# An encoder-decoder layer with cross attention: rows centred by ScalarE, and all copies of turned probabilities on ScalarE

## The chip, the core and the metric

The kernel runs on one core of a Trainium2 chip. A core has five engines that run their own queues of instructions in order and wait for each other by semaphores: TensorE (PE in the profile, with its weight loads as PEld), VectorE (DVE), ScalarE (ACT), GpSimd (POOL) and SyncE (SP), which here only issues transfers. Matrix products and transposes of TensorE land in PSUM, which has eight banks of 128 x 512 floats; everything else lives in SBUF, 128 partitions wide. The metric is the device time of one execution in microseconds, taken as the median of several runs.

## What is computed

Two batches of one encoder layer over 77 context rows and one decoder layer over 2048 rows, width 512, 16 heads of 32, feed-forward width 2048, all in float32:

```python
x = src                                    # (2, 77, 512)
x = x + mha(ln(x, n1), ln(x, n1), enc_in, enc_out, rel_bias)
x = x + relu(ln(x, n2) @ ff1.T + b1) @ ff2.T + b2
memory = x
y = tgt                                    # (2, 2048, 512)
y = y + mha(ln(y, n1), ln(y, n1), sa_in, sa_out, rel_bias + causal)
y = y + mha(ln(y, n2), memory, ca_in, ca_out, cross_bias)     # the cross attention
h = ln(y, n3)
y = y + relu(h @ ff1.T + b1) @ ff2.T + b2

def ln(x, s, b):
    m = mean(x); v = mean((x - m) ** 2)    # over the 512 of a row
    return (x - m) * rsqrt(v + 1e-6) * s + b
```

The change touches two norms of the decoder, n2 ahead of the cross attention and n3 ahead of the feed-forward part, and the softmax probabilities of the cross attention.

## The kernel before

The decoder's rows are cut into eight blocks of 512 (two batches of four), and each block into four tiles of 128 rows. The first part of the span, to about 1757 us, is causal self-attention with the encoder's stages between its units; in its second half (about 923 to 1215 us) the cross attention of block 0 is put between the units as well (`first_cross`). From there on runs the feed-forward part, 56 slots a block. In every slot the generator `cross(x + 1)` first adds its stages for the next block, and then `ff_slot` adds 1/56 of this block's feed-forward products. The first 28 slots of a block are `first_product`, the others `second_product`; both use Strassen-like sums of sub-matrices, so that VectorE and GpSimd add and subtract 128 x 512 pieces (`minus`, L1090, and others) while TensorE multiplies.

The order of instructions is written out by hand: no scheduler moves anything, so each engine executes its part of the program in the order in which the program emits it. An engine whose next instruction waits holds back all of its later ones.

**The norms.** `norm_stages` gives three stages for a tile of rows. `stats` lets VectorE take mean and variance (L740, L741), add epsilon (L742), and GpSimd raise the sum to the power -1/2 (L743). `center` has VectorE subtract the mean and multiply by that factor (L749), from the rows `y` in SBUF into a spare tile `xn`; then GpSimd adds to `y`, in place, the bias row of the coming product (L750). `turned` has TensorE transpose `xn` into one PSUM bank (L755) and ScalarE apply scale and shift on the way to SBUF, four 128 x 128 pieces (L758). In `cross`, the three stages of tile t of n2 are in the slots t, t + 2 and t + 4; q products (`q_group`, L765) follow in slots 9 to 12. For n3, they are 13, 15 and 17 slots after the slot where the tile's attention starts, 14 + 7t. At slot 0, `sums_n` also puts four sums (L1090) on GpSimd.

**The attention of a tile.** `attend_stages` gives scores (L780, four PSUM banks, then L789 and L790 on VectorE), exp (L793), sums (L798, L799), the normalization on GpSimd (L804), `turned`, the product with v (L821, copied by L825), and the output product (L830, added to y by L831). `turned` transposes the 16 heads' probabilities into four banks (L810, 16 transposes), and copies each bank to SBUF: two by VectorE (L812) and two by ScalarE (L814), in turns. In the feed-forward part only four banks rotate for all of this, because the other four hold the feed-forward products, so the scores of the next tile, one slot on, use the same banks again.

**The feed-forward evacuations** share the queues: `first_product` ends with a copy by ScalarE (L1313), or with an addition by VectorE (L1316), and for a finished piece two relus by ScalarE (L1319). ScalarE's copy L1340 and VectorE's L1341 and L1346 to L1348 belong to `second_product`, with GpSimd's additions L1351 and L1270 beside them.

Of the kernel before, what the change touches and what calls it, by code (L numbers as in the profile page):

```python
# [10 lines left out]
F32 = mybir.dt.float32  # L11
AF = mybir.ActivationFunctionType
ALU = mybir.AluOpType
# [4 lines left out]
P = 128  # L18
B, T, S, D = 2, 2048, 77, 512
# [35 lines left out]
def tile_encoder_decoder(ctx: ExitStack, tc: tile.TileContext, ins, out):  # L55
    nc = tc.nc
# [20 lines left out]
    def vec(name, i):  # L77
        c = _COL[name] + i
        return vecs[:, c : c + 1]
# [78 lines left out]
    with (  # L158
# [20 lines left out]
        def bank():  # L179

            i = count["bank"] % count["banks"]
            count["bank"] += 1
            return psum[:, i, :]
# [6 lines left out]
        def rows4(r):  # L190
            return slice(r * HD, (r + 1) * HD)
# [540 lines left out]
        def norm_stages(y, n, row, place, done):  # L732

            keep = {}

            def stats():
                st = sm.tile([P, 6], F32, name="bnst", tag="bnst")
                mv = sm.tile([P, 2], F32, name="cmv", tag="cmv", bufs=4)
                rs = sm.tile([P, 2], F32, name="crs", tag="crs", bufs=4)
                nc.vector.bn_stats(st, y())  # L740
                nc.vector.bn_aggr(mv, st)  # L741
                nc.vector.tensor_scalar_add(rs[:, 0:1], mv[:, 1:2], EPS)  # L742
                nc.gpsimd.tensor_tensor(rs[:, 1:2], rs[:, 0:1], mhalf[:, 0:1], ALU.pow)  # L743
                keep.update(mv=mv, rs=rs)

            def center():
                xn = keep["xn"] = place()
                mv, rs = keep["mv"], keep["rs"]
                nc.vector.tensor_scalar(xn, y(), mv[:, 0:1], rs[:, 1:2], ALU.subtract, ALU.mult)  # L749
                nc.gpsimd.tensor_tensor(y(), y(), row, ALU.add)  # L750

            def turned():
                xn, pt, dst = keep["xn"], bank(), done()
                for c in range(NC):
                    nc.tensor.transpose(pt[:, ts(c, P)], xn[:, ts(c, P)], ident)  # L755
                for c in range(NC):
                    sc, bi = vec(f"dec_{n}_s", c), vec(f"dec_{n}_b", c)
                    nc.scalar.activation(dst[:, c, :], pt[:, ts(c, P)], AF.Identity, bias=bi, scale=sc)  # L758

            return stats, center, turned  # L760
# [7 lines left out]
        def attend_stages(q, kTc, v, y, biased, pr, pts, place, w_o, bi=None):  # L768


            prh = pr.rearrange("p (h k) -> p h k", k=S)
            by_r = pr.rearrange("p (g r k) -> p g r k", r=HC, k=S)
            keep = {}

            def score():
                mx = sm.tile([P, NC, HC], F32, name="cmx", tag="cmx", bufs=3)
                banks = [bank() for _ in range(HC)]
                for g in range(NC):
                    for r in range(HC):
                        nc.tensor.matmul(  # L780
                            banks[r][:, ts(g, S)], q(g)[rows4(r)], kTc[rows4(r), g, :], start=True, stop=True
                        )
                for r in range(HC):
                    s = banks[r][:, : NC * S].rearrange("p (g k) -> p g k", k=S)
                    d = by_r[:, :, r, :]
                    if biased:
                        nc.vector.tensor_tensor(d, s, bi[r] if bi else d, ALU.add)
                        s = d
                    nc.vector.tensor_reduce(mx[:, :, r], s, AX.X, ALU.max)  # L789
                    nc.vector.tensor_tensor(d, s, mx[:, :, r, None].to_broadcast([P, NC, S]), ALU.subtract)  # L790

            def exp():
                nc.scalar.activation(pr, pr, AF.Exp)  # L793

            def sums():
                su = sm.tile([P, H], F32, name="csu", tag="csu", bufs=2)
                ri = sm.tile([P, H], F32, name="cri", tag="cri", bufs=2)
                nc.vector.tensor_reduce(su, prh, AX.X, ALU.add)  # L798
                nc.vector.reciprocal(ri, su)  # L799
                keep["ri"] = ri  # L800

            def normalize():
                ri = keep["ri"]
                nc.gpsimd.tensor_tensor(prh, prh, ri[:, :, None].to_broadcast([P, H, S]), ALU.mult)  # L804

            def turned():
                for g in range(NC):
                    pt = bank()
                    for r in range(HC):
                        nc.tensor.transpose(pt[:S, ts(r, P)], prh[:, g * HC + r, :], ident)  # L810
                    if g % 2:
                        nc.vector.tensor_copy(pts(g), pt[:S, :])  # L812
                    else:
                        nc.scalar.copy(pts(g), pt[:S, :])  # L814

            def times_v():
                ot = bank()
                for g in range(NC):
                    for r in range(HC):
                        h = g * HC + r  # L820
                        nc.tensor.matmul(  # L821
                            ot[rows4(r), ts(g, P)], v[:, ts(h, HD)], pts(g)[:, ts(r, P)], start=True, stop=True
                        )
                keep["oT"] = place()
                nc.scalar.copy(keep["oT"], ot)  # L825

            def out():
                mm, oT = bank(), keep["oT"]
                for c in range(NC):
                    nc.tensor.matmul(mm, oT[:, ts(c, P)], w_o[:, c, :], start=(c == 0), stop=(c == NC - 1))  # L830
                nc.vector.tensor_tensor(y(), mm, y(), ALU.add)  # L831

            return score, exp, sums, normalize, turned, times_v, out

        def first_cross():
# [713 lines left out]
```

## Time and profile before

| what | us |
|---|---|
| median of 3 runs | 2880.58 (2879.85 to 2881.13) |
| the profiled execution, its time | 2880.44 |
| the profiled execution, its span | 2878.70 |
| TensorE busy | 2827.8 |
| VectorE busy | 2033.3 |
| ScalarE busy | 1296.5 |
| GpSimd busy | 737.3 |
| L749, centring on VectorE, 64 of them | 0.54 to 1.53 each |
| L812, copies on VectorE, 64 of them | 0.68 each |
| L814, copies on ScalarE, 64 of them | 0.57 to 0.58 each |
| L743, the power on GpSimd, 64 of them | 0.54 to 1.11 each |

Durations and moments come from one profiled execution; moments are counted from the start of its span. A row in order of time reads: start, duration, engine, line, operation, output and inputs with the buffers' names, shapes, and how many instructions were merged into the row; in brackets how long the engine sat idle before it, and what ended that. A row of waits reads: engine and line that waited, the engine and line it waited for, the total in us, how often, and the longest. Durations of neighbours on one engine may overlap by some hundredths of a us. What `DVE pts L749` or `DVE xt L749` names is the same line with another spare tile for its output.

### The profile page before, as it was taken

Reading aid. Unit: us, or ns where it says so; the run is one execution under the profiler, and the core shown is the slowest. Engines: PE = TensorE matmul, PEld = TensorE weight load, DVE = VectorE, ACT = ScalarE, POOL = GpSimd, SP = SyncE. Lnnn points to the kernel's source line nnn. Section 1 sums busy time; section 2 is a strip of 40 time slices with the busy share of each in tenths; the row PEclk is TensorE's granted clock in tenths of the full one; section 3 lists DMA queues with packets and bytes.
Section 4 is the critical chain, followed back from the end, with each engine's and each line's share of the span. In section 5 each row is a group of like instructions: output and inputs, shape, how many; then the busy total and the mean of one; then the engine's idle time right before and its main releaser. Section 6 shows DMA issues by size and latency. Waiting matters only on the chain.

```text
span 2878.7 us, 64333 instructions
## 1 busy us (share of the span) xinstructions
PE 2827.8 (98%) x25782; PEld 2041.2 (71%) x25782; DVE 2033.3 (71%) x5550; ACT 1296.5 (45%) x2455; POOL 737.3 (26%) x573
## 2 busy tenths in 40 slices
PE   9899999999999999999999999999999999999998
PEld 5557666666666556666666677888888888888888
DVE  4767688878986678788878894666666666666645
ACT  3344465456665446555546674323232323232321
POOL 0100050200000101020000002363636363636355
PEclk9899999999999999999999999999999999999999
DMA  6413443401111502232301115454546454545365
GB/s 174 116 32 123 122 135 101 121 18 45 35 42 57 143 23 68 71 105 69 89 16 38 38 35 188 131 182 130 182 131 198 130 182 131 181 132 180 116 201 182
DMA packets 251773, 316.16 MB, mean 110 GB/s; under 512 B 29472, under 2 KB 142672, under 8 KB 251346
## 3 DMA queue, kind: packets, MB, share of 16 engines
q1 hardware_dynamic: 251474, 312.05, 35.9%
q8 instruction: 203, 3.33, 0.5%
q14 instruction: 96, 0.79, 0.1%
HBM read 273.07 MB, written 38.90 MB: 108 GB/s over the span
## 4 chain that ended last, share of the span: by engine, by line
PE 81%; DVE 8%; POOL 4%; ACT 3%; issue 3%; DMA 1%; SPq 0%; POOLq 0%; DVEq 0%; ACTq 0%
PE psum L425 17%; PE psum L371 11%; PE psum L1303 10%; PE psum L442 9%; PE psum L1332 7%; PE psum L765 4%; PE psum L215 4%; PE psum L239 4%; PE psum L251 4%; PE psum L226 3%; PE psum L830 3%; DVE pp L1090 2%; PE psum L780 1%; PE psum L810 1%; ACT pp L402 1%
## 5 line engine op out<-in xcount | busy, mean ns | idle before, releaser
L402 ACT ACTIVATE pp<-pp,nm 128x128 f32<-128x128 f32 (+15 forms) x512 | 611.6, 1201 | 265.6 <-DVE nm L397 265.3
L380 DVE TENSOR_SCALAR_CACHE_REDUCE pp<-psum 128x512 f32<-128x512 f32 (+3 forms) x1024 | 559.2, 590 | 58.2 <-PE psum L371 56.7
L425 PEld LDWEIGHTS psum<-ident,pp 128*128 128x128 f32 x4352 | 475.3, 142 | 110.1 <-DVE pp L380 50.8
L425 PE MATMUL psum<-ident,pp 128*128 128x128 f32 x4352 | 537.6, 278 | 8.3 <-DVE mx L387 3.8
L431 ACT COPY pts<-psum 128x512 f32<-128x512 f32 (+3 forms) x592 | 298.1, 575 | 474.9 <-PE psum L425 368.8
L429 DVE COPY pts<-psum 128x512 f32<-128x512 f32 (+2 forms) x544 | 330.0, 659 | 68.2 <-PE psum L425 67.9
L371 PE MATMUL psum<-kT,q 32*128 32x512 f32 (+3 forms) x2560 | 362.4, 578 | 7.1 <-ACT pts L431 4.5
L442 PEld LDWEIGHTS psum<-pts,vv 128*32 128x32 f32 x8704 | 227.3, 110 | 126.1 <-issue 117.3
L1332 PE MATMUL psum<-pp 128*128 128x128 f32 x2560 | 306.4, 276 | 1.9 <-POOL pp L1090 1.6
L1332 PEld LDWEIGHTS psum<-pp 128*128 128x128 f32 x2560 | 295.8, 192 | 17.4 <-issue 10.6
L442 PE MATMUL psum<-pts,vv 128*32 128x128 f32 x8704 | 280.9, 277 | 0.7 <-ACT pts L431 0.6
L1303 PE MATMUL psum<-vv,pp 128*128 128x256 f32 x1024 | 238.5, 381 | 0.0
L371 PEld LDWEIGHTS psum<-kT,q 32*128 32x128 f32 x2560 | 125.7, 184 | 143.6 <-issue 88.6
L1303 PEld LDWEIGHTS psum<-vv,pp 128*128 128x128 f32 x1024 | 189.8, 190 | 32.2 <-issue 8.4
L387 DVE CUSTOM_DVE_ANT_0 pp<-psum,bias 128x256 f32<-128x256 f32 (+1 forms) x512 | 195.9, 411 | 16.4 <-PE psum L371 16.4
L1090 POOL TENSOR_TENSOR pp<-pp 128x512 f32<-128x512 f32 x124 | 171.6, 1399 | 105.2 <-DMA pp<-in_dec_ff_wT_dram 91.2
L285 POOL TENSOR_TENSOR rstd<-rstd,mhalf 128x1 f32<-128x1 f32 x32 | 18.2, 570 | 668.1 <-DVE rstd L284 668.1
L1319 ACT ACTIVATE kT<-kT,vecs 128x256 f32<-128x256 f32 x192 | 87.7, 508 | 219.3 <-DVE kT L1316 219.2
L1303 PE MATMUL psum<-nT,pp 128*128 128x256 f32 x768 | 173.4, 379 | 0.0
L1303 PEld LDWEIGHTS psum<-nT,pp 128*128 128x128 f32 x768 | 145.3, 190 | 28.6 <-issue 10.2
L804 POOL TENSOR_TENSOR oT<-oT,cri 128x1232 f32<-128x1232 f32 x28 | 67.7, 2418 | 353.8 <-DVE cri L799 353.8
L1316 DVE TENSOR_TENSOR kT<-kT,psum 128x512 f32<-128x512 f32 x96 | 65.7, 686 | 119.1 <-PE psum L1303 89.7
(188 smaller groups left out, 3703.9 us busy)
## 6 DMA issues: line engine op xcount, KB each, us to landing
pp<-w_d SPq DMA_DIRECT2D x520, 256.0 KB, 2.9
pp<-in_dec_ff_wT_dram SPq DMA_DIRECT2D x112, 256.0 KB, 3.8
wqk<-in_dec_sa_in_wT_dram SPq DMA_DIRECT2D x64, 256.0 KB, 3.7
bias<-tzg SPq DMA_DIRECT2D x128, 128.0 KB, 3.7
wbig<-in_dec_sa_in_wT_dram SPq DMA_DIRECT2D x8, 1024.0 KB, 6.6
vv<-in_enc_ff_wT_dram SPq DMA_DIRECT2D x8, 1024.0 KB, 5.3
wbig<-in_dec_sa_out_wT_dram SPq DMA_DIRECT2D x8, 1024.0 KB, 6.6
vv<-y SPq DMA_DIRECT2D x32, 256.0 KB, 5.5
```

The costliest lines, as they stand in the source:

```text
L215: nc.tensor.matmul(mm, w[:, c, :], nTs[b, m][:, c, :], start=(c == 0), stop=(c == NC - 1))
L371: nc.tensor.matmul(banks[r][:, : kn * P], q[rows4(r), ts(t, P)], kT[rows4(r), g, k0 * P : (k0 + kn) * P], start=True, stop=True,)
L380: nc.vector.tensor_scalar(p[:, k0 * P : (k0 + far) * P], s[:, : far * P], 1.0, None, ALU.mult, ALU.max, accum_out=st["mx"][:, r, c : c + 1],)
L387: nc.vector.tensor_tensor_reduce(p[:, (i + 1) * P - w : (i + 1) * P], s[:, far * P : kn * P], biases[b, m, g][:, r, 2 * P - w :], 1.0, LOW ...
L402: nc.scalar.activation(p, p, AF.Exp, bias=nm, accum_out=to)
L425: nc.tensor.transpose(pt[:, ts(x, P)], state[n]["p"][r][:, ts(k, P)], ident)
L429: nc.vector.tensor_copy(pts[:, : len(load), :], pt[:, :w])
L431: nc.scalar.copy(pts[:, : len(load), :], pt[:, :w])
L442: nc.tensor.matmul(ot[rows4(r), t, :], vv[:, k, ts(g * HC + r, HD)], got.pop((n, k, r)), start=(k == 0), stop=(k == i),)
L1090: engine.tensor_tensor(out, a, b, ALU.subtract)
L1303: nc.tensor.matmul(mm[:, ts(f, TOK)], a[:, c, ts(f, P)], b[:, c, :], start=fresh and f == 0 and c == 0, stop=c == 1, skip_group_check=True,)
L1332: nc.tensor.matmul(psum[:, bank_i, ts(col, P)], lhs[:, c, :], w[:, c, :], start=fresh and k in (0, 3) and c == 0, stop=c == 3, skip_group_ ...
```

## The change

`stats` now has GpSimd compute a third column after the power, minus the mean times the factor, in one instruction of one column. `center` is now a ScalarE activation, the identity with a scale (the factor) and a bias (that third column) for each row, in VectorE's place; the two forms give the same value, (x - m) r = x r + (-m r). GpSimd's addition to `y` thus waits for ScalarE's reading of `y`. In `turned` of the attention all four copies are ScalarE's. All else is as it was; later lines move up or down by up to two (the centring is L750, the new multiplication L744, the copies L812 in the changed kernel, GpSimd's row addition L751, evacuations L759, relus L1317 and copies L1311 of the feed-forward part).

```diff
             def stats():
...
-                rs = sm.tile([P, 2], F32, name="crs", tag="crs", bufs=4)
+                rs = sm.tile([P, 3], F32, name="crs", tag="crs", bufs=4)
                 nc.vector.bn_stats(st, y())
                 nc.vector.bn_aggr(mv, st)
                 nc.vector.tensor_scalar_add(rs[:, 0:1], mv[:, 1:2], EPS)
                 nc.gpsimd.tensor_tensor(rs[:, 1:2], rs[:, 0:1], mhalf[:, 0:1], ALU.pow)
-                keep.update(mv=mv, rs=rs)
+                nc.gpsimd.tensor_scalar(rs[:, 2:3], mv[:, 0:1], rs[:, 1:2], -1.0, ALU.mult, ALU.mult)
+                keep.update(rs=rs)
 
             def center():
                 xn = keep["xn"] = place()
-                mv, rs = keep["mv"], keep["rs"]
-                nc.vector.tensor_scalar(xn, y(), mv[:, 0:1], rs[:, 1:2], ALU.subtract, ALU.mult)
+                rs = keep["rs"]
+                nc.scalar.activation(xn, y(), AF.Identity, bias=rs[:, 2:3], scale=rs[:, 1:2])
                 nc.gpsimd.tensor_tensor(y(), y(), row, ALU.add)
...
                     for r in range(HC):
                         nc.tensor.transpose(pt[:S, ts(r, P)], prh[:, g * HC + r, :], ident)
-                    if g % 2:
-                        nc.vector.tensor_copy(pts(g), pt[:S, :])
-                    else:
-                        nc.scalar.copy(pts(g), pt[:S, :])
+                    nc.scalar.copy(pts(g), pt[:S, :])
```

## The prediction

> **What bounds the kernel now.** I read the page's busy shares and its chain first, then what TensorE (PE) waited for, then instructions in order of time around those waits.
>
> ```profile
> span 2878.7 us, 64333 instructions
> PE 2827.8 (98%) x25782; PEld 2041.2 (71%) x25782; DVE 2033.3 (71%) x5550; ACT 1296.5 (45%) x2455; POOL 737.3 (26%) x573
> ...
> PE 81%; DVE 8%; POOL 4%; ACT 3%; issue 3%; DMA 1%; SPq 0%; POOLq 0%; DVEq 0%; ACTq 0%
> ```
>
> TensorE is busy for 98%, so the change is worth what it does to TensorE's 51 us of idle time, not what it moves between VectorE (DVE) and ScalarE (ACT). What TensorE waited for, in total us, times and longest, between 1860 and 2770 us:
>
> ```profile
> PE psum L755 <- DVE xt L749: 6.5, 9, 1.1
> PE psum L755 <- DVE pts L749: 3.0, 4, 1.1
> PE psum L780 <- DVE pts L812: 2.3, 7, 0.3
> ```
>
> Both edited lines stand here: 9.5 us for the centring (L749), 2.3 us for the copies (L812). 11.8 us is all that the change can take away directly. The order in time, one block of the feed-forward part (blocks repeat every 143.9 us):
>
> ```profile
> 2036.48 0.66 PE L755 MATMUL psum<-ident,pts 128*128 128x128 f32 x4 [0.44 <-DVE pts L749]
> ...
> 2064.72 0.60 PE L755 MATMUL psum<-ident,xt 128*128 128x128 f32 x4
> ...
> 2068.14 0.66 PE L755 MATMUL psum<-ident,pts 128*128 128x128 f32 x4 [1.08 <-DVE pts L749]
> 2068.63 1.89 PE L1303 MATMUL psum<-vv,pp 128*128 128x256 f32 x8
> 2070.36 0.60 PE L755 MATMUL psum<-ident,xt 128*128 128x128 f32 x4
> ```
> ```profile
> 2034.36 0.54 POOL L743 TENSOR_TENSOR crs<-crs,mhalf 128x1 f32<-128x1 f32 x1
> ...
> 2060.41 0.55 POOL L743 TENSOR_TENSOR crs<-crs,mhalf 128x1 f32<-128x1 f32 x1
> 2060.92 1.27 POOL L1090 TENSOR_TENSOR vv<-nT 128x512 f32<-128x512 f32 x1
> 2062.27 1.33 POOL L1090 TENSOR_TENSOR vv<-nT,vv 128x512 f32<-128x512 f32 x1
> ...
> 2066.02 0.55 POOL L743 TENSOR_TENSOR crs<-crs,mhalf 128x1 f32<-128x1 f32 x1
> 2066.53 1.26 POOL L750 TENSOR_TENSOR vv<-vv,row_sa_bv 128x512 f32<-128x512 f32 x1
> ```
> ```profile
> 2069.74 0.91 ACT L1319 ACTIVATE kT<-kT,vecs 128x256 f32<-128x256 f32 x2 [4.70 <-DVE kT L1316]
> 2070.55 1.49 ACT L758 ACTIVATE pp<-psum,vecs 128x128 f32<-128x128 f32 x4
> 2071.92 0.59 ACT L1313 COPY kT<-psum 128x512 f32<-128x512 f32 x1
> ```
>
> The reader sees a 1.08 us wait in the norm ahead of the queries (n2, second of four row tiles): GpSimd (POOL) reaches the power at 2066.02 only, after four sums of 1.27, VectorE centres after it, TensorE transposes after that. This form occurs in six blocks (6 x 1.08 = 6.5); the other 3.0 us are 0.43 in each of seven blocks, in the norm after the attention (n3, third tile), again behind a late power, at 2034.36. So what bounds both places is GpSimd, and the centring is the last link.
>
> **Part 1, VectorE's centring goes (64 x L749).** By line it takes 0.54 us at least, 1.45 in the median of those from vv. VectorE's own work hides behind TensorE; the gain is the last link only: 1.48 us at 2066.60, with 0.03 from the power's end to it and 0.06 from its end to the transposes.
>
> **Part 2, ScalarE's centring.** No row has it. ScalarE's exp with one per-partition operand takes 390 ns at 128x128 and 710 at 128x512 (groups by shape), so 0.32 us more for 384 columns; L758 with two such operands takes 475 (median, 128x128). 475 + 320 = 0.80 us. Ends: 0.59 (L1313's copy of 128x512) and 1.23 (exp over 128x1232). I take 0.80, the two rows with the same operands. The last link is 0.65 us shorter.
>
> **Part 3, GpSimd's extra multiplication (64, on 128x1, right after the power).** The trace has none. Nearest by shape is the power itself, 0.55; the other end is the page's memset of 128x1, 0.10. It needs the power's result: dependent GpSimd instructions leave a gap (the sum at 2062.27 starts 0.08 after its input's end at 2062.19), independent ones overlap by 0.03, so 0.11 more. I take 0.55 + 0.11 = 0.66; the low end is 0.21. It is in GpSimd's queue ahead of the four sums too, and of the row additions L750, which now wait for ScalarE's reading instead of VectorE's.
>
> **Part 4, n2 worked out.** GpSimd: tile 0's multiplication stands before the sums, tile 1's behind its power, so tile 1's factor comes at 2066.57 + 2 x 0.66 = 2067.89. Centring to 2068.72, transposes at 2068.78. TensorE is ready at 2068.14 - 1.08 = 2067.06: wait 1.72.
> ScalarE's queue in the changed program is: centre 1, the pair of relus (0.81 to the next), four evacuations L758 of tile 0 (1.37), centre 2, a copy (0.49), four evacuations of tile 1, centre 3. The relus and evacuations behind centre 1 now wait for GpSimd with it. Centre 2 can start by this queue at 2067.92 + 0.72 + 0.81 + 1.37 = 2070.82 (0.72 because neighbours overlap by some 0.08). Its factor: the row addition of tile 0 from 2068.72 (1.26), power, multiplication: 2071.15. It ends at 2071.95, transposes 2072.01; TensorE is ready 2.22 after the last transposes (2068.14 to 2070.36), at 2071.00: wait 1.01. Centre 3 starts 0.72 + 0.49 + 1.37 later, at 2073.73, transposes at 2074.59, ready at 2074.23: wait 0.36.
> Sum 3.09 against 1.08: +2.01 in six blocks, **+12.1**. What is late next: the query products L765 waited 0.12 for the last evacuation (2076.58 to 2076.70); TensorE now arrives later than ScalarE, **-0.7** in six.
> With the low end, 0.21: waits 0.82, 0.68 and 0.36, +0.78 in six, +4.7. So even a nearly free multiplication leaves n2 no faster.
>
> **Part 5, n3.** Third tile: power's end 2034.90 + 0.66 + 0.03 + 0.80 + 0.06 = 2036.45, ready at 2036.04: wait 0.41 instead of 0.44, **-0.2** over seven; with 0.21 the wait goes, -3.0. The other three tiles have their centred rows 1 us and more ahead (the nearest, the fourth: power's end 2048.46, rows 2050.0, transposes 2051.12). ScalarE idles there (4.35 us before L825 at 2034.12), so L825 behind the centring slips by 2.2 us, to 2036.3; its reader L830 starts at 2038.76.
>
> **Part 6, the copies (64 x L812 to ScalarE).** 0.58 us each (L814), 0.49 apart when queued; TensorE makes a bank in 0.49. So ScalarE ends 0.8 us behind the last transpose, and the next scores L780 come 1.7 us behind it: the seven waits go, **-2.3**. Where a relu is in front (1842.90, two L814 in 1.22) the four end 0.6 us before L780.
>
> **Part 7, the first block, inside self-attention.** 8 x 0.80 + 8 x 0.57 = 11 us more on ScalarE between 923 and 1215 us: 0, since ScalarE idles 3 to 10 us ahead of most groups there and TensorE waits for neither line. 11 us if that cover were gone; VectorE's relief brings no more than the 4.3 us that TensorE waited in that stretch at all. Table, DMAs and SP's queue are unchanged.
>
> **Sum.** 12.1 - 0.7 - 0.2 - 2.3 = +8.9 with the multiplication at 0.55; 4.7 - 0.7 - 3.0 - 2.3 = -1.3 at 0.10. The profiled execution took 2880.44 (span 2878.7 and 1.74 around it), the median is 2880.58, so either base serves: 2889.3, and 2879.1 at the low end. I forecast 2889, by the row of the same engine and shape.
>
> A rule speaks against the row I chose. The Trainium skill, GPSIMD Engine Reference, section Instruction dispatch, puts the cost of entering an instruction at tens of cycles, so the power's 0.55 would be mostly its arithmetic, and a product of one column would cost an estimated 0.1 us. By that the sum is -1.3; no row here shows such a product.
>
> **Rivals.**
> *Cheap multiplication, no change.* The two ends give 10.2 us for 0.45 us of multiplication, 23 us per us; so at 0.10 to 0.40 us the sum lies between -1.3 and +5.6. For it: GpSimd's sums of 384 columns take 1.007 and of 512 take 1.27, which leaves 0.22 at no column; against: the only 128x1 arithmetic takes 0.55. Time 2882.
> *Faster.* Mechanism: ScalarE's centring in n2 is so short that its queue keeps up. The three waits are 3 x centring + 2 x (multiplication with gap) - 0.96; with 0.21 they fall below today's 1.08, and the total below -5.8, once the centring is under 0.55. At 0.50 the total is -6.6: 2874. For it: ScalarE's 256-column relu from SBUF takes 0.51. Against: exp over 512 takes 0.71 with one operand fewer.
> *Much slower.* ScalarE's waiting for GpSimd reaches the exponentials in the first block: all of its 11 us, on top of +8.9: 2900. Against: there the factor is ready a slot earlier, GpSimd idling 8 to 10 us at a time.
>
> **How the numbers follow.** A measurement here tells about 0.2% (5.8 us) from no change. Forecast +6 to +14: 0.44; much slower 0.06; cheap multiplication 0.38; faster 0.12. So slower 0.50, same 0.38, faster 0.12. The forecast's own range is 2886.4 to 2894. The range that leaves out 2 in 10 reaches through the cheap case (2879, and some 4 us for what I charged nothing) to half of the faster one at 2875, and up to 2895.
>
> **What would show it.** TensorE's waits for L812 gone; L755 waiting for ScalarE (L750 there) in n2 at the second, third and fourth tile, 1.7, 1.0 and 0.4; the new L744 on GpSimd at about 0.55; ScalarE waiting for GpSimd some 2 to 3 us at tile 1. Wrong if L744 takes 0.2 or less, if the centring differs from 0.80, or if L755 waits only at the second tile.

## The result, and the profile after

| | us |
|---|---|
| before, median of the runs beside it (7 each) | 2881.13 (2877.09 to 2882.96) |
| after, median | 2870.03 (2868.08 to 2871.86) |
| ratio, with its 95% interval | 0.9963 (0.9951 to 0.9975) |
| after, the profiled execution and its span | 2870.03 and 2868.2 |

The change makes the kernel 0.37% faster: 2880.58 x 0.9963 is 10.7 us less. The forecast was 2889, 8 us slower, and its range began at 2875. From the page of the kernel after, the head, the busy shares and the chain that ended last:

```profile
span 2868.2 us, 64539 instructions
...
PE 2821.6 (98%) x25782; PEld 2036.2 (71%) x25782; DVE 1930.3 (67%) x5422; ACT 1371.7 (48%) x2583; POOL 741.8 (26%) x637
...
PE 90%; DVE 3%; ACT 3%; POOL 2%; DMA 1%; issue 1%; SPq 0%; POOLq 0%; DVEq 0%; ACTq 0%
```

VectorE gave up 103 us of work, ScalarE took over 75, and TensorE is still busy for 98% of the span. Its own busy time fell by 6.2 us, although it executes the same 25782 instructions: part of the gain hides in what the profile calls busy. What TensorE waited for between 1860 and 2770 us, in total us, times and longest:

```profile
PE psum L756 <- ACT xt L750: 7.1, 12, 1.1
PE psum L756 <- ACT pts L750: 3.6, 6, 1.1
```

The waits for the copies are gone, and the waits for centred rows add up to 10.7 where they were 9.5. By this view alone the change would be worth 1.1 us. The norm ahead of the queries (n2) in the same block as before, TensorE in order of time:

```profile
2060.70 0.60 PE L756 MATMUL psum<-ident,xt 128*128 128x128 f32 x4
...
2064.12 0.66 PE L756 MATMUL psum<-ident,pts 128*128 128x128 f32 x4 [1.08 <-ACT pts L750]
...
2067.00 0.66 PE L756 MATMUL psum<-ident,xt 128*128 128x128 f32 x4 [0.50 <-ACT xt L750]
...
2069.58 0.66 PE L756 MATMUL psum<-ident,xt 128*128 128x128 f32 x4 [0.19 <-ACT xt L750]
...
2073.53 3.60 PE L766 MATMUL psum<-pp,wqk 128*128 128x512 f32 x8
```

There are three waits now, where there was one. On GpSimd, the power, the new product, and the row addition that follows:

```profile
2062.30 0.55 POOL L743 TENSOR_TENSOR crs<-crs,mhalf 128x1 f32<-128x1 f32 x1
2062.95 0.27 POOL L744 TENSOR_SCALAR crs<-cmv,crs 128x1 f32<-128x1 f32 x1
2063.17 1.27 POOL L751 TENSOR_TENSOR vv<-vv,row_sa_bv 128x512 f32<-128x512 f32 x1
```

The product takes 0.27, with a gap of 0.10 ahead of it (the power ends at 2062.85). From a power's start to the next instruction it is 0.87 now and was 0.51 (2066.02 to 2066.53), so the product costs GpSimd's queue 0.36. And ScalarE's queue:

```profile
2063.25 0.81 ACT L750 ACTIVATE pts<-vv,crs 128x512 f32<-128x512 f32 x1 [2.37 <-POOL crs L744]
2063.97 0.89 ACT L1317 ACTIVATE kT<-kT,vecs 128x256 f32<-128x256 f32 x2
2064.77 1.48 ACT L759 ACTIVATE pp<-psum,vecs 128x128 f32<-128x128 f32 x4
2066.14 0.81 ACT L750 ACTIVATE xt<-vv,crs 128x512 f32<-128x512 f32 x1
```

The centring takes 0.81. The second one starts at 2066.14, 0.8 us after GpSimd has its factor (the product of 2065.05 ends at 2065.32): here ScalarE's queue is the last link, with the relus and evacuations that queued up behind the first centring's wait.

**Where the time went.** Up to the start of the feed-forward part the two profiled executions agree (1757.41 before, 1756.80 after). From there to the end, before took 1121.3 us and after 1111.4, 9.9 less. The waits as printed don't add up to that, so each place is measured by TensorE's steps: from the start of one group of matmuls to the start of a later one, against the same stretch where nothing waits.

The largest term is at the scores of each block's fourth tile, which take the banks that hold the third tile's turned probabilities. Before, TensorE in order of time:

```profile
2153.78 0.44 PE L780 MATMUL psum<-pts,bias 32*128 32x77 f32 x2
2154.56 0.45 PE L780 MATMUL psum<-pts,bias 32*128 32x77 f32 x4 [0.34 <-DVE pts L812]
2155.16 1.11 PE L780 MATMUL psum<-pts,bias 32*128 32x77 f32 x26
2156.20 2.05 PE L1332 MATMUL psum<-pp 128*128 128x128 f32 x16
```

After, the same place:

```profile
2150.51 1.13 PE L781 MATMUL psum<-pts,bias 32*128 32x77 f32 x32
2151.57 1.60 PE L1330 MATMUL psum<-pp 128*128 128x128 f32 x12
```

The 32 matmuls of one tile take 1.06 us to the next group in the kernel after, and took 2.42 before: the stall was 1.36, of which the profile printed 0.34 as idle. The rest stood in the rows as busy time: the three rows add up to 2.00, while 32 matmuls in one run take 1.13. The likely reason is that each time a wait cuts the group, the passage of the matmuls last issued stands as busy time of its own, where in one run it lies under the next ones. The view of groups had it, before and after (busy us, mean ns, then idle us with what ended it):

```profile
L780 PE MATMUL psum<-pts,bias 32*128 32x77 f32 x896 | 37.7, 279 | 3.4 <-DVE pts L812 2.3
```
```profile
L781 PE MATMUL psum<-pts,bias 32*128 32x77 f32 x896 | 31.7, 277 | 0.0
```

The 896 matmuls of this shape are busy for 6.0 us less, which is part of the gain, and their idle time falls from 3.4 to 0.0.

Why the copies were late is in VectorE's queue of the kernel before, in order of time:

```profile
2147.39 5.18 DVE L1090 TENSOR_TENSOR pp<-pp,kT 128x512 f32<-128x512 f32 x3
2152.49 0.41 DVE L1341 TENSOR_TENSOR oT<-psum,oT 128x256 f32<-128x256 f32 x1
2152.83 0.68 DVE L740 BATCH_NORM_STATS2 bnst<-vv 128x6 f32<-128x512 f32 x1
...
2153.83 1.27 DVE L812 COPY pts<-psum 77x512 f32<-77x512 f32 x2
```

The transposes into the four banks had ended at 2152.07. But three sums held VectorE to 2152.5, and the statistics of n3's second tile came next, so the two copies ran at 2153.83 to 2155.10, while TensorE wanted those banks for scores at 2153.78.

| per block, feed-forward part | before | after | times | us |
|---|---|---|---|---|
| scores of the fourth tile, start to next group | 2.42 | 1.06 | 7 | -9.5 |
| n3's third tile, step into its transposes | 2.49 | 1.88 | 7 | -4.3 |
| n2, first to fourth tile's transposes | 7.80 | 8.88 | 6 | +6.5 |
| n2, last transposes to the query products | 4.18 | 3.95 | 6 | -1.4 |
| end of the fourth tile's scores to its transposes L810 | 14.32 | 14.25 | 7 | -0.5 |

That is -9.2 of the 9.9. The second row is TensorE's matmuls L1332 at 2033.99 to L755 at 2036.48 before, against 1.88 where nothing waits (2016.18 to 2018.06). The start of the feed-forward part differs by a few us between executions (1753.2 to 1761.0 among the profiles of this study, with the first part of the span much the same program), so no more than that is accounted for.

### The profile page after: what moved, and what is told of

It reads as the page before. It is cut to its first block, busy times and chain, and to the rows that moved or that the text cites. A ratio compares the mean times of both kernels' runs of the same rounds, so it can differ in the third digit from the quotient of the medians.

```text
span 2868.2 us, 64539 instructions
## 1 busy us (share of the span) xinstructions
PE 2821.6 (98%) x25782; PEld 2036.2 (71%) x25782; DVE 1930.3 (67%) x5422; ACT 1371.7 (48%) x2583; POOL 741.8 (26%) x637
## 4 chain that ended last, share of the span: by engine, by line
PE 90%; DVE 3%; ACT 3%; POOL 2%; DMA 1%; issue 1%; SPq 0%; POOLq 0%; DVEq 0%; ACTq 0%
PE psum L425 17%; PE psum L1330 12%; PE psum L1301 11%; PE psum L371 11%; PE psum L442 9%; PE psum L828 4%; PE psum L766 4%; PE psum L215 4%; PE psum L239 4%; PE psum L251 4%; PE psum L226 3%; PE psum L811 2%; PE psum L781 1%; PE psum L819 1%; ACT pp L402 1%
## 5 line engine op out<-in xcount | busy, mean ns | idle before, releaser
L1330 PEld LDWEIGHTS psum<-pp 128*128 128x128 f32 x2560 | 295.8, 192 | 17.4 <-issue 12.1
L1317 ACT ACTIVATE kT<-kT,vecs 128x256 f32<-128x256 f32 x192 | 86.9, 500 | 192.0 <-DVE kT L1314 192.0
```

The lines of the kernel that those rows point to most:

```text
L1330: nc.tensor.matmul(psum[:, bank_i, ts(col, P)], lhs[:, c, :], w[:, c, :], start=fresh and k in (0, 3) and c == 0, stop=c == 3, skip_group_ ...
```

## The experiments

All were timed against the kernel before in the same series: 2880.74 for the first four, 2882.19 for the last four. The theory: the copies brought the gain, because VectorE's queue made them late, and n2 gave part of it back. The rival: the gain is the centring's, through VectorE's relief. A second question was who makes n2 wait, GpSimd's product, ScalarE's queue or the sums ahead of both.

**The copies alone.** The kernel before, with only this:

```diff
-                    if g % 2:
-                        nc.vector.tensor_copy(pts(g), pt[:S, :])
-                    else:
-                        nc.scalar.copy(pts(g), pt[:S, :])
+                    nc.scalar.copy(pts(g), pt[:S, :])
```

> Theory A (the banks): the gain is the scores L780, which stood 2.42 us instead of 1.06 in each of seven blocks because VectorE's two copies came late; 7 x 1.36 = 9.5, so 2881.1 - 9.5 = 2871.6 with the copies alone. L755 keeps its waits, 6 x 1.08 and 7 x 0.43. Theory B (the row of waits is the whole cost, and the gain came from taking the centring off VectorE): 7 x 0.33 = 2.3, so 2878.8.

Measured: 2871.97, ratio 0.9972 (0.9962 to 0.9983). The copies alone bring 8.8 us by the medians and 8.1 by the ratio, of 10.7, and the two intervals overlap. The scores are busy for 31.7 us and idle for 0.0, as in the kernel after. TensorE's waits in this kernel, total us, times and longest:

```profile
PE psum L755 <- DVE xt L749: 4.3, 4, 1.1
PE psum L810 <- POOL oT L804: 3.7, 7, 0.5
PE psum L755 <- DVE pts L749: 2.2, 2, 1.1
```

Two more things stand there. The seven waits of 0.43 in n3, which were expected to stay, are gone though VectorE still centres; the paragraph on n3 below says what it was. And there are seven new waits of 0.5 at the fourth tile's L810, for the normalization L804 on GpSimd, which the kernel after doesn't have. In this kernel VectorE centres a tile of n3 ahead of the sums of the exponentials (VectorE in order of time):

```profile
2156.99 0.54 DVE L749 TENSOR_SCALAR xt<-vv,cmv,crs 128x512 f32<-128x512 f32 x1
...
2161.74 1.42 DVE L798 TENSOR_REDUCE csu<-oT 128x16 f32<-128x1232 f32 x1
```

In the kernel after the same sums start at 2160.89, with the scores 0.10 earlier (2150.51 against 2150.61). So the sums are 0.75 later where VectorE centres; from the scores' start to the transposes of the probabilities it is 16.06 here (2150.61 to 2166.67) and 15.31 after (2150.51 to 2165.82):

```profile
2166.67 1.97 PE L810 MATMUL psum<-ident,oT 128*77 128x128 f32 x16 [0.53 <-POOL oT L804]
```
```profile
2165.82 1.97 PE L811 MATMUL psum<-ident,oT 128*77 128x128 f32 x16
```

That is 0.75 in seven blocks, 5.3 us, that centring on ScalarE takes away once the copies are ScalarE's: it pays for what n2 loses, +6.5 - 1.4 = 5.1, and brings no more than that. A measure without the start of the feed-forward part says the same: from the first scores of one block to those of the next (mean of six, in the profiled execution) it is 143.90 before, 142.58 here and 142.61 after.

**The centring alone.** The kernel after, with the copies shared as before:

```diff
-                    nc.scalar.copy(pts(g), pt[:S, :])
+                    if g % 2:
+                        nc.vector.tensor_copy(pts(g), pt[:S, :])
+                    else:
+                        nc.scalar.copy(pts(g), pt[:S, :])
```

> Theory A: n2 costs 6 x 0.71 more, n3 saves 7 x 0.43, the query products save 6 x 0.23, the scores' stall shrinks by at most 0.35 in seven blocks because VectorE has one instruction fewer ahead of the copies: 4.3 - 3.0 - 1.4 - 2.4 = -2.5, so 2878.6 (2881 if the stall stays). Theory B: most of the gain, 2871 to 2873.

Measured: 2879.45, ratio 0.9998 (0.9989 to 1.0007): worth nothing that this measurement tells. The group of the scores shows that they still stall (busy us, mean ns, then idle us with what ended it):

```profile
L781 PE MATMUL psum<-pts,bias 32*128 32x77 f32 x896 | 37.7, 279 | 1.3 <-DVE pts L813 0.5
```

TensorE is busy there for 37.7, as before, 6.0 above the undisturbed 31.7, and the stretch is 2.11 long (2153.92 to 2156.03), 1.05 above the undisturbed 1.06. So 7.3 us of stall remain in seven blocks, of which the profile prints 0.5 as waiting for the copies and 1.3 as idle in all. n2's waits are 1.08, 0.50 and 0.20, as in the kernel after, and those of n3 are back at 0.41, where none were expected. Blocks repeat every 144.06 us.

**Is it VectorE's order?** The kernel before, with the statistics of n3's four tiles emitted at the end of their slots, so behind the copies where a slot has both; nothing goes to another engine:

```diff
-            bias_1 = None
+            bias_1, behind = None, []
...
-                for k, f in zip((13, 15, 17), fs):
+                behind.append((at + 13, fs[0]))
+                for k, f in zip((15, 17), fs[1:]):
...
+            for n, f in behind:
+                plan[n].append(f)
```

> Kernel before, with the statistics of n3 (1.0 us on VectorE) emitted behind the copies of the same slot instead of ahead of them; both copies stay on VectorE. Theory A in the form that VectorE's queue, not its speed, makes the copies late: they come 1.0 us earlier, the scores lose 0.36 instead of 1.36 in seven blocks, 2881.1 - 7.0 = 2874.1. If VectorE itself is too slow for the copies: 2881.

Measured: 2872.53, ratio 0.9972 (0.9962 to 0.9982). VectorE's queue of this kernel, in order of time:

```profile
2151.84 1.27 DVE L812 COPY pts<-psum 77x512 f32<-77x512 f32 x2
2153.03 0.67 DVE L740 BATCH_NORM_STATS2 bnst<-vv 128x6 f32<-128x512 f32 x1
```

TensorE there:

```profile
2152.80 1.47 PE L780 MATMUL psum<-pts,bias 32*128 32x77 f32 x32
2154.20 2.05 PE L1332 MATMUL psum<-pp 128*128 128x128 f32 x16
```

The copies run at once behind L1341 and the scores take 1.40 instead of 2.42, with VectorE doing the same work as before. So it was not how much VectorE had to do but that 1.0 us of statistics stood ahead of the two copies. This kernel has the new wait of 0.5 at L810 too (seven times), and blocks repeat every 142.68 us.

**The waits of n3.** They went in three kernels that have little in common: after, the copies alone, and this one. What these share is on GpSimd, ahead of the power of n3's third tile. The addition L1351 there, in the kernel before:

```profile
2029.87 2.84 POOL L1351 TENSOR_TENSOR vv<-vv,oT 128x512 f32<-128x512 f32 x1
...
2034.36 0.54 POOL L743 TENSOR_TENSOR crs<-crs,mhalf 128x1 f32<-128x1 f32 x1
```

And in the kernel after, where the line is L1349:

```profile
2026.51 1.72 POOL L1349 TENSOR_TENSOR vv<-vv,oT 128x512 f32<-128x512 f32 x1
```

Exactly seven of the 56 additions take 2.83 to 2.85 in the kernel before, one in each block that waited, and seven in the kernel with the centring alone, which still waits; none takes over 1.73 in the three that do not. In the two that wait, VectorE's copies run beside this addition (2029.70 to 2030.97 here); with the copies ahead of it, in the third experiment, it takes 1.26, and without them on VectorE 1.71. So the copies cost TensorE twice: through the bank, and by an addition on GpSimd that is 1.1 longer with them beside it. What in that stretch of VectorE's queue holds GpSimd is not shown: at 2153.78 a sum on GpSimd ran beside the same copies in 1.26.

**The product's price.** The kernel after, with the new product emitted twice (the second writes the same value again):

```diff
                 nc.gpsimd.tensor_scalar(rs[:, 2:3], mv[:, 0:1], rs[:, 1:2], -1.0, ALU.mult, ALU.mult)
+                nc.gpsimd.tensor_scalar(rs[:, 2:3], mv[:, 0:1], rs[:, 1:2], -1.0, ALU.mult, ALU.mult)
```

> Kernel after, with GpSimd's product of one column made twice, so that it takes some 0.69 with its gaps instead of 0.34, near the 0.66 of the prediction. If GpSimd's chain sets n2 as the prediction had it: the three waits go from 1.09 + 0.50 + 0.19 to about 3.0, +1.2 in six blocks, and n3's third tile waits some 0.3 in seven: 2870.0 + 9 = 2879. If ScalarE's queue alone sets them: 2870.

Measured: 2874.93, ratio 0.9982 (0.9973 to 0.9991), 4.9 above the kernel after (5.5 by the ratios), between the two cases. Blocks repeat every 143.30 us, 0.69 more than after. TensorE at n2's second to fourth tile:

```profile
2067.32 0.66 PE L757 MATMUL psum<-ident,pts 128*128 128x128 f32 x4 [1.80 <-ACT pts L751]
...
2070.20 0.66 PE L757 MATMUL psum<-ident,xt 128*128 128x128 f32 x4 [0.50 <-ACT xt L751]
...
2072.78 0.66 PE L757 MATMUL psum<-ident,xt 128*128 128x128 f32 x4 [0.20 <-ACT xt L751]
```

The first wait grows by 0.72, which is twice the 0.36 of one product: tile 0's stands ahead of the sums, tile 1's behind its power. 6 x 0.72 = 4.3 of the 4.9. The other two stay as they were, though one more product lies between each tile's factor and the next: what sets them is ScalarE's queue, as its rows in the kernel after had it.

**Taking GpSimd's sums out of the way.** If the four sums L1090 ahead of tile 1's power are what makes n2 late, centring and product cost nothing there without them. The sums are needed later, so they were put two and two behind the second and the fourth tile's power:

```diff
-        def sums_n():
-            minus(gp, of_n("T1"), of_n("12"), of_n("11"))
-            minus(gp, of_n("T2"), of_n("22"), of_n("T1"))
-            minus(gp, of_n("T3"), of_n("22"), of_n("12"))
-            minus(gp, of_n("T4"), of_n("21"), of_n("T2"))
+        def sums_n(n):
+            if n == 1:
+                minus(gp, of_n("T1"), of_n("12"), of_n("11"))
+                minus(gp, of_n("T2"), of_n("22"), of_n("T1"))
+            elif n == 3:
+                minus(gp, of_n("T3"), of_n("22"), of_n("12"))
+                minus(gp, of_n("T4"), of_n("21"), of_n("T2"))
...
-            if n == 0:
-                sums_n()
+            sums_n(n)
```

In the kernel before:

> Kernel before, with the four sums of a block's start split: T1 and T2 behind the second tile's power on GpSimd, T3 and T4 behind the fourth's. If n2's 1.08 us is GpSimd's queue: the wait goes in six blocks, 2880.7 - 6.5 = 2874.2. If it is VectorE's centring (1.45 us) that is late: no more than 6 x 0.4 = 2.4 is gained, 2878.3. If T2 comes late for the third product: a new wait at L1303 and no gain.

Measured: 2872.46, ratio 0.9963 (0.9951 to 0.9976). The six waits of 1.08 are gone, those of n3 and of the copies stay (3.1 and 2.3 in total). TensorE at n2's first and fourth tile and at the query products (one of their eight falls outside this view):

```profile
2066.68 0.60 PE L755 MATMUL psum<-ident,xt 128*128 128x128 f32 x4
...
2073.18 0.60 PE L755 MATMUL psum<-ident,xt 128*128 128x128 f32 x4
...
2077.07 3.17 PE L765 MATMUL psum<-pp,wqk 128*128 128x512 f32 x7
```

The gain of 9.7 is more than the 6.5 that the printed waits had promised. By the steps it is 6.50 and 3.89 here, where the kernel before has 7.80 and 4.18: 1.59 in six blocks, 9.5. The printed idle time understated this stall too. In the kernel after:

> Kernel after, with the same split. GpSimd's factors come early, so all three waits of n2 go if ScalarE's queue then keeps ahead, 6 x 1.79 = 10.7: 2870.0 - 10.7 = 2859.3. If ScalarE's queue sets the second and third wait whatever GpSimd does: only 6 x 1.09 = 6.5, 2863.5.

Measured: **2856.08, ratio 0.9908 (0.9893 to 0.9924)**, the fastest of all, 14 us below the kernel after (16 by the ratios). Between 1860 and 2770 us no wait of TensorE is left in the view, and n2's four groups follow each other by 2.16, 2.17 and 2.29:

```profile
2058.18 0.60 PE L756 MATMUL psum<-ident,xt 128*128 128x128 f32 x4
...
2060.34 0.60 PE L756 MATMUL psum<-ident,pts 128*128 128x128 f32 x4
...
2062.51 0.60 PE L756 MATMUL psum<-ident,xt 128*128 128x128 f32 x4
...
2064.80 0.66 PE L756 MATMUL psum<-ident,xt 128*128 128x128 f32 x4
```

From the first of them to the query products it is 10.57 here and 12.83 after: 6 x 2.26 = 13.6, where the printed waits were 10.7. So all three waits hung on the four sums, and here too the gain is above what the waits had promised (2859.3 was expected).

**The centring of n2 back on VectorE.** The kernel after, with n2's centring as before and no product for it; n3's centring and all copies stay ScalarE's:

```diff
-                nc.gpsimd.tensor_scalar(rs[:, 2:3], mv[:, 0:1], rs[:, 1:2], -1.0, ALU.mult, ALU.mult)
+                if n == "n3":
+                    nc.gpsimd.tensor_scalar(rs[:, 2:3], mv[:, 0:1], rs[:, 1:2], -1.0, ALU.mult, ALU.mult)
...
-                nc.scalar.activation(xn, y(), AF.Identity, bias=rs[:, 2:3], scale=rs[:, 1:2])
+                if n == "n3":
+                    nc.scalar.activation(xn, y(), AF.Identity, bias=rs[:, 2:3], scale=rs[:, 1:2])
+                else:
+                    nc.vector.tensor_scalar(xn, y(), keep["mv"][:, 0:1], rs[:, 1:2], ALU.subtract, ALU.mult)
```

> Kernel after, with n2's centring back on VectorE and without its product on GpSimd; n3's centring and the copies stay on ScalarE. If the change's cost lies in n2 alone: the waits go back from 1.79 to 1.08, and the query products wait some 0.2 again: 2870.0 - 4.3 + 1.4 = 2867.1. If the two centrings cannot be told apart: 2870.

Measured: 2865.92, ratio 0.9941 (0.9928 to 0.9953), 4.1 below the kernel after (6.3 by the ratios), with six waits of 1.08 as the only ones. The table's rows for n2 (+6.5 - 1.4) had given 5.1. So the centring by ScalarE helps in n3 and, with the sums ahead of it, hurts in n2.

**The copies alone, with the sums moved.** The kernel before, with the diff of the first experiment and that of the moved sums together, and VectorE's centring.

> Copies alone on ScalarE, centring on VectorE, with the split sums: 2872.0 - 6.5 = 2865.5 if the wait in n2 is GpSimd's queue, with the waits of L810 for GpSimd's normalization (3.7) staying. Compared with the other split it tells whether the centring on ScalarE is worth anything once n2 waits for nothing: 6 us by these sums.

Measured: 2862.22, ratio 0.9930 (0.9918 to 0.9943). Against the fastest kernel, from which it differs by the centring alone, it is 6.1 slower; its only waits are the seven of 0.5 at L810. Once n2 doesn't wait, centring on ScalarE is a gain. Blocks repeat every 140.90 us here and 140.34 in the fastest, so 3.9 in seven blocks is shown: the 0.75 of the fourth tile, less what n2 still gives back. Of the rest, 2.0 is the start of the feed-forward part in the two profiled executions (1758.53 and 1756.55), within what it varies by.

## Why the prediction was wrong

**Part 6, "the seven waits go, -2.3", is the largest step that failed.** The mechanism was right, the size was read off the printed idle time, 7 x 0.33. The stall was 7 x 1.36 = 9.5, as the scores' length of 2.42 against 1.06 shows, and the copies alone brought 8.8 on the whole. The row needed was in the profile of before: the same line's rows of the other tiles show 32 matmuls in 1.13 us. With it went the bound "11.8 us is all that the change can take away directly", a sum of printed waits. By itself this step would not have turned the sign: 8.9 - 7.2 is +1.7. With the price of the product in n2 (5.6, the next two paragraphs) it is -3.9, and with n3 (4.1, the one behind them) -8.0.

**Part 3, the product at 0.55 and 0.11.** Measured 0.27 in the median (0.27 to 0.72) and 0.10, so 0.36 on GpSimd's queue instead of 0.66. I took the nearest row by shape, the power; the product takes half as long. The Trainium skill, GPSIMD Engine Reference, section Instruction dispatch, speaks of tens of cycles for entering an instruction, from which I had estimated 0.1 us; the measurement lies between this and the row I chose. By the two medians a power takes 0.28 more than a product.

**Part 4, n2.** Forecast waits of 1.72, 1.01 and 0.36; measured 1.08, 0.50 and 0.19. With 0.36 for the product the same working gives 1.12, 0.68 (by ScalarE's queue) and 0.36, which is +6.5 in six blocks, and by TensorE's steps it was +6.5. That the first wait takes two products is shown by the doubled product. One link was wrong: "the row addition of tile 0 from 2068.72", that is, behind the centring. It follows the product at once (2063.17), because it adds to a tile whose centring is long done; so GpSimd had the second factor early, and ScalarE's queue set the second wait as well as the third. The query products gave back 1.4, forecast 0.7.

**Part 5, n3, "wait 0.41 instead of 0.44".** Wrong: it went, and with the copies alone too. I followed the power back to GpSimd's queue and stopped there; the 2.84 of L1351 two rows further up, against 1.26 to 1.72 for all its others, was the cause, and the removed copies ran beside it. Forecast -0.2, measured -4.3.

**Parts 1, 2 and 7.** The centring on ScalarE takes 0.81 (forecast 0.80). VectorE's relief was costed at nothing beyond the last link; it turned out worth 0.75 in seven blocks, but only once the copies had gone: before that the fourth tile's scores were held up themselves, and no wait for L804 shows behind them. The first block is unchanged, as forecast: the feed-forward part starts 0.6 us earlier, within what it varies by.

**The sum.** From +8.9 to -10.7: the copies account for 7.2 of the difference, n2 for 5.6 (12.1 to 6.5, nearly all of it the product's price), n3 for 4.1, the query products for 0.7 and the fourth tile for 0.5; 1.5 is left to the accounting and to the start of the feed-forward part.

**The rivals.** "Cheap multiplication, no change" had the product right (0.10 to 0.40) and the time wrong, since it used the same 2.3 for the copies. "Faster" gave 2874, 4 us above the measured median, by a mechanism that did not occur, so that its number is luck: it asked for a centring under 0.55 and three waits below 1.08 in n2, and n2 got slower. "Much slower" did not occur. The chance of 0.12 for faster was too low for a reason that can be named: all four cases shared the printed waits as the most that could be gained.

## What to carry to other kernels

Measure what a stall costs by the length of the whole group of matmuls against the same group where nothing waits, not by the idle time printed in front of it: here 1.36 a block against 0.34, and with the centring alone 7.3 us in all against 0.5. When a copy that frees a PSUM bank is late, look first at what stands ahead of it in its engine's queue; moving 1.0 us of statistics behind two copies brought as much as giving the copies to another engine. And before an engine is relieved of the last link of a chain, move the work that makes the first link late: the change is worth 11 us as it stands, and 16 (2872.46 to 2856.08) once four sums are put behind the powers.

## What was not expected of the hardware

A product of one column on GpSimd takes 0.27 us in the median of 64, a power of one column 0.55, and the product starts 0.10 behind the end of the power that it reads (2062.85 to 2062.95). The GpSimd addition L1351 of 128 x 512, 1.26 to 1.73 elsewhere, took 2.83 to 2.85 in seven places where VectorE's copies out of PSUM and its sums ran beside it; which of them held it is open. And the identity with a scale and a bias per row on ScalarE takes 0.81 for 128 x 512, on a chain where VectorE's form took 1.48, and 0.54 to 1.53 over the span.
